# GRU gates of a fused graph network: h_n and i_n as four 64x64 corner matmuls

## The chip, the cores and the metric

The kernel runs on one core of a Trainium2 chip. The metric is the device time of one execution in microseconds: 815.14 us, the median of three runs (815.1 to 816.52). The profiled execution spans 813.9 us.

## The reference

A graph of 4096 nodes with 64 features each, and a 4096 x 4096 adjacency matrix of zeros and ones, passes through four layers. Each layer computes `x = x + layer(relu(layernorm(x)), adj)`. Layers 0, 1 and 3 are a decayed neighbour sum, a hyperbolic attention and a hyperbolic midpoint. The change lies in layer 2, which applies a gated graph convolution twice:

```
m = adj @ (x @ W)
gi = m @ wih.T + bih
gh = x @ whh.T + bhh
i_r, i_z, i_n = jnp.split(gi, 3, axis=-1)
h_r, h_z, h_n = jnp.split(gh, 3, axis=-1)
r = jax.nn.sigmoid(i_r + h_r)
z = jax.nn.sigmoid(i_z + h_z)
n = jnp.tanh(i_n + r * h_n)
return (1.0 - z) * n + z * x
```

The gates r and z need the sum of a product with x and a product with m. The candidate n needs the two products apart, because r multiplies only h_n.

## The kernel before, in words

The nodes are cut into four quarters of 1024. The adjacency matrix stays on the chip in fp8. It is converted while layer 0 runs; a check of the fp32 original (the tile `whole`, function `checks`) goes along on VectorE in the background through layers 0 to 2, because the fast path holds only for zeros and ones.

The program consists of the streams of the four layers and of chains of small operations between them. `stream0` ends at about 280 us and `stream1` at about 494. `layer2` runs twice: step 0 to about 602 us, step 1 to about 705. `layer3` ends on TensorE at about 793, and a tail on VectorE and ScalarE follows.

In `layer2` the sum adj @ x is made for each quarter, with x split into three bf16 parts (`hm` holds two of them side by side, `lo` the third). The multiplication with W is folded into the gate weights by `load_gates` once per step. `take2` then places the result m beside x: the tile `mx[0]` has x on partitions 0 to 63 and m on 64 to 127 for one chunk of 512 nodes, and `mx[1]` has them the other way round for the other chunk. `gates` (line 1509) makes the GRU of one quarter from these two tiles. So it is called eight times, four quarters by two steps.

The weight tile `gw` has for each chunk four blocks of 64 columns, for r, z, h_n and i_n. Its 128 rows meet the rows of `mx`, so that one matmul adds the product with x and that with m. For h_n the rows that meet m are zero, and for i_n those that meet x are zero (`pack_consts` leaves these blocks at zero). A gate is therefore two matmuls with 128 rows and 64 columns, one per chunk; the first writes partitions 0 to 63 of the result, the second 64 to 127. The tile `rz` holds r in its first bank and z in its second, the tile `ih` holds i_n in its first and h_n in its second.

The order of the work is made at build time by a planner, `Weave`. Each chain is a generator that yields operations; each operation is booked on a model of its engine with an estimated duration. While the sums of `layer2` are emitted, `draw` looks which yielded operations could begin by the model, and places them there. A chain goes on to its next operation only when the one before is placed. `book_pe` (line 964) holds the estimates for TensorE: a matmul that uses only half of the rows or columns is booked at half the time, and a switch between such matmuls and full ones gets a surcharge. The hardware queues then run in the emitted order and wait on semaphores.

In `gates` the order of the chain is: first gate r, then h_n (line 1526), then the sigmoid for r on ScalarE (1528), then gate i_n (1529) and gate z (1530), then on VectorE `(h_n + b) * r` and the addition of i_n (1531 and 1532), then the sigmoid for z, the tanh and the blend with x.

Of the kernel before, what the change touches and what calls it, by code (L numbers as in the profile page):

```python
# [18 lines left out]
P = 128  # L19
D = 64  # L20
NH = 2
CW = 512
# [578 lines left out]
def names(*aps):  # L601
    return [a.tensor.name for a in aps if isinstance(a, bass.AP)]


class Weave:
# [52 lines left out]
    def free(self, ps):  # L658
        k = ps.tensor.name
        self.banks[self.kind.pop(k)].append(self.used[k][0])  # L660
# [131 lines left out]
def fast_kernel(ctx: ExitStack, tc: tile.TileContext, t: dict, out: bass.AP, flag: bass.AP):  # L792
# [30 lines left out]
    def two(name):  # L823
        return weave.take(2, lambda: psp.tile([P, 2 * CW], F32, tag="two", name=name, bufs=2))
# [4 lines left out]
    def b2(name, shape=(P, QB, D), dtype=F32):  # L829
        return b2p.tile(list(shape), dtype, tag="b2", name=name)  # L830
# [57 lines left out]
    def w(name, a=0, b=None):  # L888
        s = L.at[name]
        return W[:, s.start + a:s.stop if b is None else s.start + b]  # L890
# [73 lines left out]
    def book_pe(o, lhsT, rhs, passes):  # L964
        k, m, n = lhsT.shape[0], math.prod(lhsT.shape[1:]), math.prod(rhs.shape[1:])
        tiled = k < P or m < P
        dur = max(0.42e-3 * n * passes * (0.5 if tiled else 1.0), 0.09)
        if passes > 1 and not tiled:
            dur += 0.05 if passes == 2 else 0.075
        weave.book("P", dur + ((0.18 if passes == 4 else 0.115) if tiled != weave.tiled else 0.0), names(lhsT, rhs), names(o))  # L970
        weave.tiled = tiled

    def mm(o, lhsT, rhs, start=True, stop=True):
        weave.wait(names(lhsT, rhs), names(o))
        book_pe(o, lhsT, rhs, 4 if lhsT.dtype == F32 else 1)
        nc.tensor.matmul(o, lhsT, rhs, start=start, stop=stop, skip_group_check=True)  # L976

    def turn4(o, src):
        book_pe(o, src, ident, 2)
        nc.tensor.transpose(o, src, ident)  # L980

    def PE(ins, run, dur, kinds=()):
        return Op("P", dur, names(*ins), (), run, kinds)
# [525 lines left out]
    def gates(q, step):  # L1509

        lo, hi = slice(0, D), slice(D, P)
        mx, xT = state.pop((step, q))
        gw, gb = gate_w[step], w(f"gb{step + 1}")
        rz, ih = [None], [None]
        assert ("gates", step) in DONE

        def gate(ps, half, i):
            if ps[0] is None:
                ps[0] = two("rz" if ps is rz else "ih")
            o = ps[0][:, half * CW:(half + 1) * CW]  # L1520
            for c in (0, 1):
                k = (4 * c + i) * D
                mm(o[lo if c == 0 else hi, :], gw[:, k:k + D], mx[c])

        yield PE(mx, lambda: gate(rz, 0, 0), 0.9, [2, 2])
        yield PE(mx, lambda: gate(ih, 1, 2), 0.9, [2])
        r = b2("r", (P, CW))
        yield AC.activation(r, rz[0][:, :CW], AF.Sigmoid, bias=gate_b[:, 2 * step:2 * step + 1])
        yield PE(mx, lambda: gate(ih, 0, 3), 0.9)
        yield PE(mx, lambda: gate(rz, 1, 1), 0.9)  # L1530
        yield DV.scalar_tensor_tensor(r, ih[0][:, CW:], gb[:, 5:6], r, op0=ALU.add, op1=ALU.mult)
        yield DV.tensor_tensor(r, r, ih[0][:, :CW], ALU.add)
        free(ih[0])
        z = b2("z", (P, CW))
        yield AC.activation(z, rz[0][:, CW:], AF.Sigmoid, bias=gate_b[:, 2 * step + 1:2 * step + 2])
        free(rz[0])
        yield AC.activation(r, r, AF.Tanh, bias=gb[:, 2:3])
        yield DV.tensor_tensor(xT, xT, r, ALU.subtract)
        yield DV.tensor_tensor(xT, xT, z, ALU.mult)
        yield DV.tensor_tensor(xT, xT, r, ALU.add)  # L1540
        return xT

    def post2a(q):
        x = yield from gates(q, 0)
        yield AC.activation(x, x, AF.Relu)
        ps = yield from to_nm(x, 1 if q < NQ - 1 else 2)
        yield from split3(ps, 1.0, *parts(3, q))
        DONE.add((3, q))
        yield from spill2(q, 1, x)

    def post2b(q):
        o = yield from gates(q, 1)
        DONE.add(("gates", q))
        kind = 1 if q < NQ - 1 else 2

        def run():
            ps = bank(kind, "ps_o")
            for j in range(4):
                turn4(ps[:, j * P:(j + 1) * P], o[:, j * P:(j + 1) * P])
            return ps  # L1560
        ps = yield PE([o], run, 0.6, [kind])
        yield DV.scalar_tensor_tensor(X[q], blocks(ps), 0.0, X[q], op0=ALU.max, op1=ALU.add)
        free(ps)
        yield from pre3(q, kind)
# [321 lines left out]
```

## Time and profile before

| | |
|---|---|
| time, median of three | 815.14 us |
| TensorE busy (matmul) | 776.2 us, 95% |
| VectorE busy | 638.4 us, 78% |
| ScalarE busy | 397.4 us, 49% |
| instructions of gate matmuls (rz and ih) | 64 and 64, 128*64, 128x512 f32 |
| busy time of rz and ih | 16.8 and 15.3 us |

A line of the profile names the engine (PE is TensorE's matmuls, PEld its weight loads, ACT ScalarE, DVE VectorE, SP the queue that issues transfers), the source line, the operation, and "out<-in" with the tiles' names. For a matmul "128*64" stands for the rows and columns of the weights in use. Line 976 is the helper that issues every matmul, and 781 the one for all VectorE and ScalarE operations, so the tile names tell them apart. In the view over time the first two numbers are the start and the length in microseconds; brackets hold the idle time before the operation and what ended it. An fp32 matmul appears as two instructions. Matmuls overlap in the pipeline, so the distance between starts says more than the lengths.

### The profile page before, as it was taken

How to read it: one execution, taken by the hardware profiler on the slowest of the kernel's cores; microseconds unless marked ns; L12 is line 12 of the kernel's file. 1: busy time of each engine (PE TensorE's matmuls, PEld its weight loads, DVE VectorE, ACT ScalarE, POOL GpSimd, SP SyncE). 2: the span in 40 equal slices, each digit the busy share in tenths (PEclk: the TensorE clock that was granted, in tenths of full speed). 3: DMA queues.
4: the chain of work that ended last, by engine and by line, in shares of the span. 5: the costliest groups of instructions: out<-in, count | busy, mean ns of one | idle time of the engine just before them, and what ended most of it. 6: DMA issues, size and time to landing. Idle time of an engine off the chain costs nothing.

```text
span 813.9 us, 12101 instructions
## 1 busy us (share of the span) xinstructions
PE 776.2 (95%) x4473; PEld 358.6 (44%) x4494; DVE 638.4 (78%) x1433; ACT 397.4 (49%) x613; POOL 61.1 (8%) x125
## 2 busy tenths in 40 slices
PE   5999999999999999999999999999999999999990
PEld 1334444444433333333333334444444444699990
DVE  6886777677678798888888888878779787774896
ACT  5655555565565657666666663022120254452333
POOL 3333232230000000000000000000000000000000
PEclk9999999999999999999999999999999999999995
DMA  9999999998301032022022016797879900000010
GB/s 220 151 176 168 201 160 192 196 161 186 104 14 39 0 118 65 0 91 65 0 66 91 0 33 239 287 319 229 283 263 356 273 23 4 2 2 1 2 41 17
DMA packets 43954, 98.39 MB, mean 121 GB/s; under 512 B 5104, under 2 KB 20464, under 8 KB 43888
## 3 DMA queue, kind: packets, MB, share of 16 engines
q1 hardware_dynamic: 25888, 78.98, 29.0%
q0 software_dynamic: 15840, 14.42, 18.9%
q10 hardware_dynamic: 2160, 4.14, 1.4%
q8 instruction: 37, 0.61, 0.3%
q14 instruction: 29, 0.24, 0.1%
HBM read 135.54 MB, written 5.24 MB: 173 GB/s over the span
## 4 chain that ended last, share of the span: by engine, by line
PE 90%; DVE 6%; ACT 1%; issue 1%; DMA 1%; SPq 0%; DVEq 0%; ACTq 0%
PE acc L976 54%; PE cnt L976 14%; PE score L976 14%; PE rz L976 2%; DVE sig L781 2%; PE ih L976 1%; PE ps_t L980 1%; PE ps_l L976 1%; DMA whole<-in_adjT 1%; PE ps_kq L976 1%; DVE ss L781 1%; DVE nt L781 1%; ACT sig L781 1%; PE ps_n L980 1%; DVE rc L781 0%
## 5 line engine op out<-in xcount | busy, mean ns | idle before, releaser
L781 ACT ACTIVATE sig<-score,fatt_add,fatt_mul 128x1024 f32<-128x1024 f32 x128 | 147.9, 1200 | 85.4 <-PE score L976 84.8
L781 DVE TENSOR_TENSOR sig<-sig,A 128x1024 f32<-128x1024 f32 x128 | 151.3, 1221 | 38.7 <-ACT sig L781 37.9
L781 DVE SCALAR_TENSOR_TENSOR whole<-whole 128x1024 f32<-128x1024 f32 x128 | 153.2, 1218 | 6.0 <-DMA whole<-in_adjT 5.6
L781 ACT ACTIVATE w<-cnt 128x512 int16<-128x512 f32 x198 | 111.2, 595 | 89.9 <-PE cnt L976 88.7
L976 PE MATMUL score<-qd,kT 64*128 64x512 f32 x512 | 128.2, 617 | 0.0
L976 PE MATMUL acc<-sig,S 128*64 128x512 f32 x512 | 125.4, 606 | 1.5 <-DVE sig L781 1.4
L976 PE MATMUL acc<-A,hm 128*128 128x512 fp8e4 x512 | 115.6, 379 | 0.8 <-DVE X L781 0.8
L976 PEld LDWEIGHTS <-hm 128*128 128x128 bf16 x768 | 73.5, 98 | 90.7 <-issue 10.5
L976 PE MATMUL cnt<-A,ftri 128*128 128x512 fp8e4 x256 | 97.9, 385 | 8.3 <-ACT A L781 8.3
L976 PE MATMUL cnt<-A,fupd 128*128 128x512 fp8e4 x248 | 95.6, 386 | 2.7 <-DVE w L781 1.6
L976 PE MATMUL acc<-S,A 128*128 128x196 bf16 x1024 | 88.2, 246 | 0.0
L976 PEld LDWEIGHTS <-A 128*128 128x128 fp8e4 x1024 | 87.1, 96 | 1.1 <-issue 0.8
L976 PEld LDWEIGHTS score<-qd,kT 64*128 64x128 f32 x512 | 43.7, 186 | 80.9 <-ACT sig L781 39.1
L781 DVE TENSOR_SCALAR w<-cnt 128x512 int16<-128x512 f32 x58 | 40.1, 691 | 45.5 <-PE cnt L976 41.1
L976 PE MATMUL acc<-w,hm 128*128 128x512 bf16 x235 | 71.0, 379 | 0.9 <-issue 0.2
L860 POOL DMA_DIRECT2D A<-in_adjT x110 | 59.3, 541 | 119.7 <-DMA A<-in_adjT 118.8
L976 PEld LDWEIGHTS acc<-sig,S 128*64 128x64 f32 x512 | 30.4, 136 | 82.7 <-issue 39.5
L976 PEld LDWEIGHTS <-lo 128*64 128x64 bf16 x768 | 36.9, 109 | 58.4 <-issue 36.4
L976 PE MATMUL acc<-A,lo 128*64 128x512 fp8e4 x512 | 59.3, 380 | 0.0
L781 ACT ACTIVATE mt<-acc 64x512 f32<-64x512 f32 x32 | 18.9, 591 | 66.2 <-PE acc L976 39.6
L976 PEld LDWEIGHTS <-fupd 128*128 128x128 bf16 x248 | 24.4, 98 | 46.0 <-issue 24.3
L1647 POOL MEMSET S<- 128x4 bf16 x8 | 0.9, 116 | 550.6 <-PE ps_l L976 505.4
(185 smaller groups left out, 649.5 us busy)
## 6 DMA issues: line engine op xcount, KB each, us to landing
whole<-in_adjT SPq DMA_DIRECT2D x128, 512.0 KB, 7.0
A<-in_adjT POOLq DMA_DIRECT2D x110, 128.0 KB, 13.2
qd<-qs SPq DMA_DIRECT2D x16, 128.0 KB, 3.0
mx<-gs SPq DMA_DIRECT2D x16, 128.0 KB, 8.1
xT<-gs SPq DMA_DIRECT2D x8, 256.0 KB, 7.6
x<-in_x SPq DMA_DIRECT2D x6, 256.0 KB, 6.1
xs<-x SPq DMA_DIRECT2D x4, 256.0 KB, 4.8
qs<-qT ACTq DMA_DIRECT2D x4, 256.0 KB, 6.3
```

Source lines behind the costliest of these rows:

```text
L781: return fn(*args, **kw)
L860: nc.gpsimd.dma_start(A8[q][b // 2][:, b % 2, :], a)
L976: nc.tensor.matmul(o, lhsT, rhs, start=start, stop=stop, skip_group_check=True)
L980: nc.tensor.transpose(o, src, ident)
L1647: nc.gpsimd.memset(S3[q, c][:, :, 3 * e:], 1.0)
```

## The change

h_n and i_n are no longer made with the zero rows. Each is now a product of 64 rows (those of x alone, or those of m alone) with 64 columns. Two gates by two chunks give four such matmuls: their inputs lie on the lower or the upper 64 partitions, and so do their outputs, and the four take all four combinations. The function `news` issues them one after the other in one step of the chain, ahead of the sigmoid for r, and the separate step for i_n disappears. The intention is that the four corners of the array work at the same time. `book_pe` now books a matmul with few rows and few columns at a quarter instead of half.

```
-        dur = max(0.42e-3 * n * passes * (0.5 if tiled else 1.0), 0.09)
+        dur = max(0.42e-3 * n * passes * (0.5 if tiled else 1.0) * (0.5 if k < P and m < P else 1.0), 0.09)
...
+        def news():
+
+            ih[0] = two("ih")
+            for c, (x, m) in enumerate(((lo, hi), (hi, lo))):
+                o = lo if c == 0 else hi
+                for own, half, i in ((x, 1, 2), (m, 0, 3)):
+                    k = (4 * c + i) * D
+                    mm(ih[0][o, half * CW:(half + 1) * CW], gw[own, k:k + D], mx[c][own, :])
+
         def gate(ps, half, i):
             if ps[0] is None:
-                ps[0] = two("rz" if ps is rz else "ih")
+                ps[0] = two("rz")
...
         yield PE(mx, lambda: gate(rz, 0, 0), 0.9, [2, 2])
-        yield PE(mx, lambda: gate(ih, 1, 2), 0.9, [2])
+        yield PE(mx, news, 0.9, [2])
         r = b2("r", (P, CW))
         yield AC.activation(r, rz[0][:, :CW], AF.Sigmoid, bias=gate_b[:, 2 * step:2 * step + 1])
-        yield PE(mx, lambda: gate(ih, 0, 3), 0.9)
         yield PE(mx, lambda: gate(rz, 1, 1), 0.9)
```

## The prediction, made before the result was known

> **What bounds the kernel now.** I read the busy shares first, then the chain that ended last, and then one gate call instruction by instruction.
>
> ```profile
> PE 776.2 (95%) x4473; PEld 358.6 (44%) x4494; DVE 638.4 (78%) x1433; ACT 397.4 (49%) x613; POOL 61.1 (8%) x125
> ...
> PE 90%; DVE 6%; ACT 1%; issue 1%; DMA 1%; SPq 0%; DVEq 0%; ACTq 0%
> PE acc L976 54%; PE cnt L976 14%; PE score L976 14%; PE rz L976 2%; DVE sig L781 2%; PE ih L976 1%; PE ps_t L980 1%; PE ps_l L976 1%; DMA whole<-in_adjT 1%; PE ps_kq L976 1%; DVE ss L781 1%; DVE nt L781 1%; ACT sig L781 1%; PE ps_n L980 1%; DVE rc L781 0%
> ```
>
> An average over stages settles nothing, so the next view cuts the span at layer 2 (494 to 602 and 602 to 705), layer 3 (to 793.2) and the tail. The first numbers are the length of the stretch and TensorE's busy time.
>
> ```profile
> 494.00:602.00 108.00, 108.00 (x635) 47.50 (x631) 87.41 (x161) 23.76 (x41) 0.00 (x0) 1.00 0.84 281
> 602.00:705.00 103.00, 101.73 (x626) 48.18 (x626) 84.30 (x212) 32.98 (x58) 0.46 (x4) 1.00 0.44 146
> 705.00:793.20 88.20, 88.18 (x1020) 86.85 (x1016) 66.17 (x266) 31.41 (x86) 0.47 (x4) 1.00 0.03 11
> ```
>
> TensorE is idle 1.3 us in the 211 us of layer 2 and not at all in layer 3, and the chain runs through the gate matmuls (rz, ih) themselves. So a microsecond taken from TensorE in layer 2 should come off the end, if it is not lost again in a wait. The eight gate calls start at 537, 548, 573, 597, 638, 649, 677 and 702 us. This is the first:
>
> ```profile
> 536.82 1.08 PE L976 MATMUL rz<-mx,g 128*64 128x512 f32 x4
> 537.72 1.89 PE L976 MATMUL ih<-mx,g 128*64 128x512 f32 x8
> 537.97 0.69 ACT L781 ACTIVATE r<-rz,gate_b 128x512 f32<-128x512 f32 x1 [3.51 <-PE rz L976]
> 539.44 1.03 PE L976 MATMUL rz<-mx,g 128*64 128x512 f32 x4
> 539.74 0.75 DVE L781 SCALAR_TENSOR_TENSOR r<-ih,W,r 128x512 f32<-128x512 f32 x1 [2.60 <-PE ih L976]
> 540.30 1.03 PE L976 MATMUL acc<-A,lo 128*64 128x512 fp8e4 x8
> ```
>
> An fp32 matmul shows as two instructions, so "ih x8" is four matmuls. Starts, not durations, tell the price, since the matmuls are pipelined: ih begins at 537.72 and the next group at 539.44, so two gates of two matmuls cost 1.72 us, 0.86 a gate. In that time two matmuls run side by side, one in each half of the columns.
>
> **What the Trainium skill says.** TensorEngine Tiling, "Tiling Modes": with 64 rows and 64 columns there are four tiles which work independently, twice as many as with 128 rows and 64 columns. The trace shows the pair form on the rows (score) and on the columns (rz, ih, lo), but no 64x64 matmul. The same section ("Key Properties") says that a change of tiling mode drains TensorE. The trace agrees and prices it, below. The same page, "Gotcha 1: PSUM Pressure", says that different row tiles cannot use the same PSUM bank at one time. Here each bank gets the top rows' result on one half of its partitions and the bottom rows' on the other; no run so far shows whether that counts as the same bank. TensorE: Matmul & The Clock Gate, "Measured speedup vs the span model", gives 10.6 times for sixteen 32x32 tiles at once, so packing in rows and columns together is not excluded.
>
> **The change, part by part.** *Removed:* in each call, h_n and i_n as four 128x64 matmuls, 1.72 us. Half of their weights are zeros, since h_n needs only the rows of x and i_n only those of m. *Added:* four 64x64 matmuls in the four corners, again 8 instructions of 512 columns. If all four run together this is one pair time, 0.86 us; if only two do, 1.72 us. I take 0.86: pairs in rows and pairs in columns each overlap fully in this trace, and each half of the partitions receives its two results in two different banks, as score's pair does.
>
> *Mode switches.* rz before and after stay 128x64, so the corners add a switch in and one out. Layer 1 shows what one costs, since it alternates two modes:
>
> ```profile
> 292.40 1.99 PE L976 MATMUL score<-qd,kT 64*128 64x512 f32 x8
> 294.32 1.94 PE L976 MATMUL acc<-sig,S 128*64 128x512 f32 x8
> 296.18 1.99 PE L976 MATMUL score<-qd,kT 64*128 64x512 f32 x8
> ```
>
> Eight instructions should take 4 x 0.43 = 1.72 us at 0.43 a pair. Score to acc takes 1.92 and acc to score 1.86, so a switch costs 0.20 into 128-column weights and 0.14 into 64-column ones, part drain and part a first weight load that nothing hides (in the first call rz, just switched in, lasts 0.90 instead of 0.86: some 0.05 of load, so 0.10 of drain). Both new switches go to 64-column weights: 2 x 0.145 = 0.29. The bounds are 0, if this pair of modes doesn't drain, and 0.40. A clean call thus gains 0.86 - 0.29 = 0.57 us.
>
> *The wait that was hidden.* The second rz gate writes the other half of the tile that the sigmoid for r reads, and waits for that sigmoid. Two calls show it:
>
> ```profile
> 550.12 0.67 ACT L781 ACTIVATE r<-rz,gate_b 128x512 f32<-128x512 f32 x1
> 550.84 0.20 PEld L976 LDWEIGHTS rz<-mx,g 128*64 128x64 f32 x4 [0.80 <-ACT r L781]
> ...
> 678.26 1.28 ACT L781 ACT_TABLE_LOAD   x1 [2.79 <-PE rz L976]
> 679.56 0.69 ACT L781 ACTIVATE r<-rz,gate_b 128x512 f32<-128x512 f32 x1
> 680.30 1.08 PE L976 MATMUL rz<-mx,g 128*64 128x512 f32 x4 [0.44 <-ACT r L781]
> ```
>
> In the first call r runs from 537.97 to 538.66, and TensorE leaves rz at 537.72: 0.94 us, which must be covered by what stands between. Before, that was 1.72; after, it is the corners with their first switch, 0.145 + 0.86 = 1.00. It just suffices, by 0.06 and the second drain. Where ScalarE is late it doesn't: in the second call (ScalarE busy with split3 of the quarter before) r ends at 550.79, and in the seventh (a table load of 1.28 us) at 680.25. There the second rz starts where it starts now, so these two calls gain nothing. Everything behind it on TensorE, the lo matmuls of the next sum, waits along. The sixth call has i_n separate (r is late at 652.43 and the planner put other sums between); there the corners go with h_n and the gain stays.
>
> *Sum:* 6 calls x 0.57 = 3.4 us. Layer 2 has nothing else to hide it, layer 3 is TensorE from end to end, and the 20 us tail only moves. The update of r on VectorE starts about 0.7 us sooner (it waits for the last ih), and z 0.57 sooner; both hang from the gates, so the chain to the next layer shortens too. I count nothing for it, because TensorE has other sums meanwhile.
>
> *The planner's price* (book_pe): corners are booked at a quarter, 0.86 for four, without a switch. It costs nothing by itself, but the order of all later work is made from these bookings. In both steps the order of fills may shift by an operation, up to a microsecond either way by the trace (idle stretches of 1.0 at 672 and 0.6 at 680). The 128 input checks go along at their DMA's pace (7.0 us to land); five or so may slip behind, into layer 3, where VectorE is busy 66 of 88 us.
>
> **The rivals.** (a) *No switch price, or no late sigmoid:* 8 x 0.86 = 6.9 us, 808.3. For it: both modes have 64 columns. Against: every change of shape in the trace pays. Chance 0.12. (b) *The gain is swallowed:* the corners overlap, but the hidden wait appears in all calls or a shifted order opens idle stretches of about 3 us: 815. For it: the margin of 0.06 us, and ScalarE late in three of eight calls. Against: layer 2 has sums to fill with. Chance 0.15. (c) *Only two corners at a time*, because of the shared banks: 1.72 + 0.29 instead of 1.72, 8 x 0.29 = 2.3 us more, 817.4, slower than before. For it: the skill's sentence on banks, and no 64x64 matmul seen. Against: halves of partitions are as separate as in the column pairs, whose two results do share a bank. Chance 0.16.
>
> **How the numbers follow.** Forecast: 815.1 - 3.4 = 811.7, chance 0.57. Faster by over 0.2% (under 813.5) holds most of the forecast and all of (a): 0.54 + 0.12 and 0.02 of (b), 0.68. Within 0.2%: most of (b) and an edge of the forecast, 0.15. Slower: (c) and 0.01 of (b), 0.17. The range leaves out (c) and takes in (a) and (b): 808.2 to 816.2.
>
> **What would show it.** In the changed profile: an ih group of 64*64, four starts within some 20 ns and the group over after 0.86 (right) or in two rounds (c); 0.10 before and 0.05 inside at each switch; the second rz 1.0 us after the corners begin, and waits for r of up to 0.9 us in one to three calls; layer 2's TensorE time down by some 4.5 us, with a little more idle. A table load or split3 landing on more of the sigmoids would make me wrong towards (b).

## The result, and the profile after

The changed kernel takes 811.46 us (median of four runs, 811.07 to 812.75) against 815.26 us before: a ratio of 0.9953, interval 0.9936 to 0.997. A second comparison gave 811.49 against 816.47, ratio 0.9944 (0.9932 to 0.9957). Forecast were 811.7 us and a range of 808.2 to 816.2.

In some executions of one and the same kernel the clock granted to TensorE falls to half for 3.41 us in layer 1, which then takes 262.3 us instead of 260.6, so the medians of two groups of runs can differ by up to 1.7 us more or less than the kernels do. The profile before has no such stretch, the profile after has one from 292.4 to 295.8 us. In the same four microseconds, before and then after, the first bracket counts TensorE's matmuls, and the third number from the end is the granted clock as a share of full speed:

```profile
293.00:297.00 4.00, 4.00 (x20) 1.30 (x18) 3.14 (x4) 2.31 (x3) 0.00 (x0) 1.00 0.63 190
293.00:297.00 4.00, 4.00 (x14) 0.91 (x10) 2.17 (x4) 2.41 (x2) 0.00 (x0) 0.65 0.63 193
```

So I also count from the last matmul of layer 1 (494.3 us before, 495.4 after, by its start), which leaves this stretch out.

The page after, busy time and the chain that ended last:

```profile
PE 772.4 (95%) x4473; PEld 355.6 (44%) x4494; DVE 638.3 (79%) x1433; ACT 396.9 (49%) x613; POOL 60.9 (8%) x125
...
PE 85%; DVE 10%; issue 1%; ACT 1%; DMA 1%; SPq 0%; ACTq 0%; DVEq 0%
```

TensorE is busy 3.8 us less, although its layer 1 is 1.65 us longer; VectorE and ScalarE are busy as long as before. But the chain runs 10% through VectorE instead of 6%; the chain in order of time, before and then after, shows where it changes over:

```profile
734.99 23.63 PE acc L976 x278
758.74 34.46 PE acc L976 x404
793.22 0.28 ACT n L781
```

```profile
734.98 16.33 PE acc L976 x192
751.34 0.39 ACT n L781
...
752.71 2.30 DVE whole L781 x4
```

From 751 us on the changed kernel's end hangs on VectorE's queue, in which two input checks (`whole`) stand. Before, the chain stays on TensorE up to 793. The first gate call after, over time:

```profile
537.99 1.08 PE L976 MATMUL rz<-mx,g 128*64 128x512 f32 x4
538.99 1.09 PE L976 MATMUL ih<-mx,g 64*64 64x512 f32 x8
539.14 0.69 ACT L781 ACTIVATE r<-rz,gate_b 128x512 f32<-128x512 f32 x1 [3.51 <-PE rz L976]
540.01 1.08 PE L976 MATMUL rz<-mx,g 128*64 128x512 f32 x4
540.92 1.25 PE L976 MATMUL acc<-A,lo 128*64 128x512 fp8e4 x10
```

From the start of rz to that of lo it is 2.93 us, against 3.48 before: 0.55 less. The eight instructions of the corners start in two rounds of four, each round within 21 ns (538.994 to 539.014 and 539.474 to 539.495), so all four run at once. The second and the seventh call, corners and second rz:

```profile
547.75 1.09 PE L976 MATMUL ih<-mx,g 64*64 64x512 f32 x8
549.46 1.08 PE L976 MATMUL rz<-mx,g 128*64 128x512 f32 x4 [0.62 <-ACT r L781]
...
675.05 1.09 PE L976 MATMUL ih<-mx,g 64*64 64x512 f32 x8
677.28 1.08 PE L976 MATMUL rz<-mx,g 128*64 128x512 f32 x4 [1.14 <-ACT r L781]
```

Here rz follows the start of the corners after 1.71 and 2.23 us instead of 1.02, because it waits for the sigmoid. These two calls take 3.62 and 4.09 us from the first rz to its successor, and took 3.63 and 4.09 before: nothing is gained. From the starts, the eight calls sum to 25.5 us instead of 28.8, 3.3 us less.

That is not all. Between the last matmul of layer 1 and the last of layer 3 the change takes off 4.8 us (298.7 to 293.9), and the tail behind it grows from 20.9 to 21.4. So 1.4 us on TensorE need another explanation, and the tail does not only move, it also grows.

### The profile page after: what moved, and what is told of

It reads as the page before. It is cut to its first block, busy times and chain, and to the rows that moved or that the text cites. A ratio compares the mean times of both kernels' runs of the same rounds, so it can differ in the third digit from the quotient of the medians.

```text
span 810.7 us, 12099 instructions
## 1 busy us (share of the span) xinstructions
PE 772.4 (95%) x4473; PEld 355.6 (44%) x4494; DVE 638.3 (79%) x1433; ACT 396.9 (49%) x613; POOL 60.9 (8%) x125
## 4 chain that ended last, share of the span: by engine, by line
PE 85%; DVE 10%; issue 1%; ACT 1%; DMA 1%; SPq 0%; ACTq 0%; DVEq 0%
PE acc L976 51%; PE score L976 14%; PE cnt L976 13%; DVE n L781 2%; PE rz L976 2%; DVE sig L781 2%; PE ps_t L980 1%; PE ps_l L976 1%; DVE ss L781 1%; DMA whole<-in_adjT 1%; DVE nt L781 1%; PE ps_kq L976 1%; PE ih L976 1%; ACT sig L781 1%; PE ps_n L980 1%
```

## The experiments

The theory: the corners save 0.55 us in six calls, the wait for the sigmoid takes back what they save in the other two, and the planner's new order brings the 1.4 us that are left. The rival: the order makes the gain. The columns are TensorE's part from the last matmul of layer 1 to the last of layer 3, the tail behind it (both in the profiled run), input checks that VectorE runs behind the sigmoid for z of the eighth call ("late checks"), the median, and its ratio to the kernel before with the interval. The kernel before had medians of 816.71, 816.47 and 816.42 us in the three groups of runs.

| kernel | TensorE | tail | late checks | median | ratio |
|---|---|---|---|---|---|
| before | 298.7 | 20.9 | 1 | 815.26 | |
| changed | 293.9 | 21.4 | 2 | 811.46 | 0.9953 (0.9936 to 0.997) |
| wide_same_order | 297.2 | 21.6 | 2 | 815.44 | 0.9989 (0.9983 to 0.9996) |
| corners_twice | 299.2 | 21.7 | 2 | 818.15 | 1.0018 (1.0012 to 1.0025) |
| corners_old_price | 301.9 | 19.3 | 0 | 818.8 | 1.0035 (1.0025 to 1.0046) |
| z_gate_early | 292.3 | 27.0 | 7 | 816.53 | 0.9993 (0.9985 to 1.0001) |
| changed_again | 293.9 | 21.4 | 2 | 811.49 | 0.9944 (0.9932 to 0.9957) |
| z_early_same_order | 294.6 | 21.6 | 2 | 813.68 | 0.9964 (0.9951 to 0.9977) |
| corners_first_same_order | 299.7 | 21.4 | 2 | 817.14 | 1.0016 (1.0008 to 1.0024) |
| z_gate_early_7_fewer | 292.3 | 27.0 | 0 | 816.23 | 0.9997 (0.9989 to 1.0005) |
| z_gate_early_7_unbooked | 292.4 | 19.6 | 0 | 809.25 | 0.9906 (0.9891 to 0.9922) |
| corners_first_planned | 292.5 | 19.3 | 0 | 808.0 | 0.9903 (0.9887 to 0.9918) |
| old_price_z_early | 301.1 | 19.6 | 0 | 816.47 | 1.0002 (0.9992 to 1.0011) |
| i_n_after_sigmoid | 295.1 | 21.7 | 2 | 812.79 | 0.9963 (0.9949 to 0.9977) |

In two of these profiles a stretch at half clock lies behind layer 1 and so within TensorE's part: in corners_old_price from 706.4 us on, where it costs about 1.7 us by the starts, and in old_price_z_early from 684.9 us on, about 1.4 us.

**wide_same_order** takes the corners away and keeps the order:

```diff
-                    mm(ih[0][o, half * CW:(half + 1) * CW], gw[own, k:k + D], mx[c][own, :])
+                    book_pe(ih[0][o, half * CW:(half + 1) * CW], gw[own, k:k + D], mx[c][own, :], 4)
+            for half, i in ((1, 2), (0, 3)):
+                for c, o in enumerate((lo, hi)):
+                    k = (4 * c + i) * D
+                    nc.tensor.matmul(ih[0][o, half * CW:(half + 1) * CW], gw[:, k:k + D], mx[c],
...
```

> Order and planner bookings are those of the changed kernel; only the four corners are again four 128-row matmuls (1.72 us, no mode switch). Theory (the corners themselves save 0.55 us in the six clean calls and nothing in the two calls where the second rz waits for the late sigmoid): 6 x 0.55 = 3.3 us more than changed, 814.8, and the other 0.5 us of the whole gain is the planner's order. Rival (the gain came mostly from the new order, fewer mode switches and a vanished idle stretch of 1 us): about 812.

```profile
538.12 1.08 PE L976 MATMUL rz<-mx,g 128*64 128x512 f32 x4
539.02 1.89 PE L1528 MATMUL ih<-mx,g 128*64 128x512 f32 x8
540.74 1.03 PE L976 MATMUL rz<-mx,g 128*64 128x512 f32 x4
541.60 0.60 PE L976 MATMUL acc<-A,lo 128*64 128x512 fp8e4 x4
```

The call takes its 3.48 us again. TensorE's part is 3.3 us longer than in the changed kernel, as the theory had it: that is the corners' share, measured in one and the same order. The other 1.4 us between this kernel and the kernel before are the order's. Most of it is an idle stretch in the kernel before that is gone, 1.0 us by the starts:

```profile
667.36 3.84 PE L976 MATMUL acc<-A,hm 128*128 128x512 fp8e4 x17
672.04 3.40 PE L976 MATMUL acc<-A,hm 128*128 128x512 fp8e4 x15 [0.83 <-DVE X L781]
```

Layers 2 and 3 also have 42 mode switches instead of 46.

**corners_twice** issues the four corners again behind the first set, unbooked:

```diff
+            for c, (x, m) in enumerate(((lo, hi), (hi, lo))):
...
+                    nc.tensor.matmul(ih[0][o, half * CW:(half + 1) * CW], gw[own, k:k + D], mx[c][own, :],
```

> The four corners are issued a second time behind the first, with no booking, so the order stays. Theory (four at once, 0.86 us a set; the wait for the late sigmoid of 0.78 and 1.30 us in calls two and seven absorbs the second set): 6 x 0.86 + 0.08 + 0 = 5.2 us more, 816.7. Rival without absorption: 8 x 0.86 = 6.9 us, 818.4. Rival of two at a time: 8 x 1.72 = 13.8 us, 825.

```profile
537.69 1.09 PE L976 MATMUL ih<-mx,g 64*64 64x512 f32 x8
538.60 1.04 PE L1529 MATMUL ih<-mx,g 64*64 64x512 f32 x8
539.57 1.08 PE L976 MATMUL rz<-mx,g 128*64 128x512 f32 x4
```

In this call a second set costs 0.86 us, without a switch. TensorE's part is 5.3 us longer for 5.2 expected, and the rivals' 6.9 and 13.8 are far off. The median, 818.15, lies near the first rival's 818.4, but the profiled run, whose layer 1 has no stretch at half clock, took 817.06. Both ends of the theory hold: four at once, and two calls in which the second set lies in the sigmoid's wait.

**i_n_after_sigmoid** leaves order and bookings, but issues the i_n pair with z:

```diff
-                    mm(ih[0][o, half * CW:(half + 1) * CW], gw[own, k:k + D], mx[c][own, :])
+                    book_pe(ih[0][o, half * CW:(half + 1) * CW], gw[own, k:k + D], mx[c][own, :], 4)
+            pair(1, 2, (lo, hi))
...
+        def last():
+            pair(0, 3, (hi, lo))
+            gate(rz, 1, 1)
...
-        yield PE(mx, lambda: gate(rz, 1, 1), 0.9)
+        yield PE(mx, last, 0.9)
```

> Order and bookings of the changed kernel, but the two corners of i_n are issued with z, behind the place of the sigmoid, as i_n was before the change. Theory (what matters is that the four stand next to each other in TensorE's queue, which they do in seven calls; in the sixth the i_n pair runs alone and pays 0.5 to 0.9 us): changed plus 0.5 to 0.9. Rival (two pairs issued apart run one after the other): changed plus 0.86 in each of six to seven calls, 5 us or more.

```profile
537.66 1.09 PE L1530 MATMUL ih<-mx,g 64*64 64x512 f32 x8
...
646.06 1.08 PE L1530 MATMUL ih<-mx,g 64*64 64x512 f32 x4
648.92 1.08 PE L1530 MATMUL ih<-mx,g 64*64 64x512 f32 x4
```

In the first call the four still run together, although h_n and i_n are separate steps; in the sixth, where other sums stand between, each pair costs a full round. TensorE's part is 1.2 us longer, somewhat over the 0.5 to 0.9 expected, since the second pair brings its own round and switch. So "issued together" matters only as neighbourhood in TensorE's queue, and is worth 1.2 us.

**corners_old_price** books the corners at half, as the rule before did:

```diff
-        dur = max(0.42e-3 * n * passes * (0.5 if tiled else 1.0) * (0.5 if k < P and m < P else 1.0), 0.09)
+        dur = max(0.42e-3 * n * passes * (0.5 if tiled else 1.0), 0.09)
```

> Corners as changed, but booked at half instead of a quarter, so that only the planner's order differs. Theory (the matmuls make the gain, the order about 1 us either way): 811 to 812.5. Rival (the order makes it): 814 or more. To be seen as well: whether the idle stretch of 1.0 us ahead of the seventh call is back.

The theory fell: with the very same matmuls the kernel is slower than the kernel before. The idle stretch ahead of the seventh call is not back, but there are new ones. The second rz gates in calls six, seven and eight (the last lasts 1.65 us because the clock falls to half in it):

```profile
650.78 1.08 PE L976 MATMUL rz<-mx,g 128*64 128x512 f32 x4 [1.64 <-ACT r L781]
...
679.93 1.08 PE L976 MATMUL rz<-mx,g 128*64 128x512 f32 x4 [2.24 <-ACT r L781]
...
706.00 1.65 PE L976 MATMUL rz<-mx,g 128*64 128x512 f32 x4 [2.92 <-ACT r L781]
```

Believing in 0.86 us more of TensorE time, the planner put more of ScalarE's other work ahead of the sigmoid (a square in calls six and eight, a table load of 1.28 us in seven and eight). TensorE is idle 7.4 us behind layer 1, against 1.8 in the changed kernel. Whether these waits alone make it slow was tried in **old_price_z_early**, with z ahead of the corners in the same order; beside the price, its edit is that of z_early_same_order below:

> Order and bookings of corners_old_price, but the z matmuls stand ahead of the corners, so that nothing waits for the sigmoid. Theory (corners_old_price loses 0.78 + 1.80 + 2.41 + 3.09 us in such waits, against 2.1 in changed): most of that comes back, 4 to 6 us under corners_old_price, 813 to 815. Rival (the planner's other placements make it slow): 817 or more.

TensorE's part fell by 0.8 us only, the ratio from 1.0035 to 1.0002. The waits for the sigmoid went, and others of 1.8, 2.9 and 2.0 us came, at transposes and at the flag matmul (which sums up the input checks). So the rival is nearer: these waits are not the cause by themselves, since without them TensorE waits elsewhere in that plan. That the plan is bad because its price is wrong is not shown. wide_same_order speaks against it as a rule: it runs 1.72 us of work in places booked at 0.86, and is 1.4 us shorter on TensorE than the kernel before, which books these matmuls at what they take.

**z_early_same_order** and **corners_first_same_order** take the wait out of the changed kernel, its order held: z's matmuls move ahead of the corners, or the corners ahead of r and z.

```diff
+            for c in (0, 1):
+                nc.tensor.matmul(rz[0][lo if c == 0 else hi, CW:], gw[:, (4 * c + 1) * D:(4 * c + 2) * D], mx[c],
...
-        yield PE(mx, lambda: gate(rz, 1, 1), 0.9)
+        yield PE(mx, book_z, 0.9)
```

> Emitted order and bookings are those of the changed kernel, except that the two z matmuls stand ahead of the corners and so ahead of the sigmoid for r, which no matmul waits for any longer. Theory (the waits of 0.78 and 1.30 us in calls two and seven are pure loss, and the chain is not longer, since it waits for the corners in any case): 2.1 us less than changed, tail as in changed. Rival (the sigmoid, 0.86 us later, delays the chain, and TensorE waits elsewhere): no less than changed.

```diff
+            corners(raw)
+            gate(raw, 0, 0)
+            gate(raw, 1, 1)
+            gate(book, 0, 0)
...
-        yield PE(mx, lambda: gate(rz, 0, 0), 0.9, [2, 2])
-        yield PE(mx, news, 0.9, [2])
+        yield PE(mx, first, 0.9, [2, 2])
+        yield PE(mx, lambda: corners(book), 0.9)
...
-        yield PE(mx, lambda: gate(rz, 1, 1), 0.9)
+        yield PE(mx, lambda: gate(book, 1, 1), 0.9)
```

> As z_early_same_order, but the corners stand ahead of r and z. In the four calls that follow full 128x128 matmuls and are followed by 128x64 ones (one, two, five, six) this makes two mode switches out of three. Theory: 4 x 0.145 = 0.6 us less than z_early_same_order, 2.6 us less than changed. Rival (r and z come 1.0 us later, the chain is longer and the sums beside it don't cover that): 0 to 1 us more than z_early_same_order.

**changed_again** is the changed kernel itself, run beside these two:

> The changed kernel once more, so that the three beside it have the same base: 0.9953 of the kernel before, about 3.8 us less.

It took 811.49 us, 0.9944 of the kernel before. Against it the two reorderings lose 2.2 and 5.7 us by their medians; TensorE's part and tail together, which leave the stretch in layer 1 out, are 0.9 and 5.8 us longer.

Both expectations failed. The rivals hold in direction, but corners_first_same_order is 5.1 us longer on TensorE than z_early_same_order, where its rival had 0 to 1. In the first call of z_early_same_order the update of r waits for the last ih, which now ends 0.93 us later, and so does all that hangs from it, up to the transposes:

```profile
539.57 0.75 DVE L781 SCALAR_TENSOR_TENSOR r<-ih,W,r 128x512 f32<-128x512 f32 x1 [2.72 <-PE ih L976]
...
544.28 0.63 ACT L781 ACTIVATE xT<-xT 128x512 f32<-128x512 f32 x1 [1.25 <-DVE xT L781]
...
545.12 0.63 PE L980 MATMUL ps_n<-fident,xT 128*128 128x128 f32 x4 [0.32 <-DVE mx L781]
```

In changed_again the same lines stand at 538.64, 543.34 and 544.62 us, and the transposes wait for nothing. The line names mx, but xT ends at 544.91, so it is xT that ended last. The chain has about 0.45 us of slack there. A delay of 0.93 uses it up and leaves TensorE idle: six such stretches of 0.3 to 0.7 us, 0.7 us more in sum than the sigmoid's waits were. With the corners first, everything in the chain comes later by another round: eight stretches of 0.6 to 1.2 us.

**z_gate_early** lets the planner place the order r, z, corners, sigmoid:

```diff
         yield PE(mx, lambda: gate(rz, 0, 0), 0.9, [2, 2])
+        yield PE(mx, lambda: gate(rz, 1, 1), 0.9)
         yield PE(mx, news, 0.9, [2])
...
-        yield PE(mx, lambda: gate(rz, 1, 1), 0.9)
```

> Order r, z, corners, then the sigmoid for r: no matmul any longer stands behind the sigmoid. Theory (waits of 0.78 and 1.30 us are all that is lost to it, and the sums beside the chain hide its later start): 2.1 us less than changed, 809.4. Rival (the sigmoid starts 0.86 us later, so the chain to the next layer is longer and the idle time appears elsewhere): 811 to 812.

TensorE's part falls by 1.6 us: both waits for the sigmoid are gone, and one stretch of 0.7 us at 667 us is left. But the tail grows by 5.7, and the median, 816.53, is above what theory and rival said. Seven checks stand at 749 to 758 us on VectorE instead of two. **z_gate_early_7_fewer** leaves these seven instructions out and keeps their bookings; **z_gate_early_7_unbooked** drops the bookings too.

```diff
+            if n > 121:
+                op.run = lambda op=op: weave.book("D", op.dur, op.ins, op.outs)
+            yield op
```

> z_gate_early with the last seven of the 128 checks left out of the VectorE queue (their loads and bookings stay, so all else is in the same order): the check covers less of the input. Theory (its 27.0 us tail, 5.7 over the changed kernel's, comes from seven checks of 1.22 us that the planner let slip to 749 us, in front of layer 3's last chains on VectorE): the tail falls to about 20 to 21, the time to 1.5 to 2.5 us under changed. Rival (the tail comes from the order of the chains themselves): 26 us or more stay.

```diff
+            if n > 121:
+                op.dur, op.run = 0.0, lambda: None
+            yield op
```

> z_gate_early with the last seven checks neither issued on VectorE nor booked by the planner (the check covers less of the input). Leaving out the instructions alone left the tail at 27.0 us, so the seven as such are not what makes it long. Theory (their bookings made the planner put the takes of the next sums ahead of the first chain of layer 3's end, and the in-order queues then wait there for TensorE): without the bookings the tail is 21 to 22 us and the time 1.5 to 2 us under changed, about 809.7. Rival (the order of the gates puts the tail off by another way): 26 us or more stay.

The first expectation failed: without 8.5 us of work in front, the tail is the same. ScalarE's queue in z_gate_early and then in z_gate_early_7_unbooked shows why:

```profile
750.80 0.28 ACT L781 ACTIVATE n<-acc 128x130 f32<-128x130 f32 x1 [2.27 <-PE acc L976]
753.52 0.28 ACT L781 ACTIVATE n<-acc 128x130 f32<-128x130 f32 x1 [2.38 <-PE acc L976]
756.24 0.28 ACT L781 ACTIVATE n<-acc 128x130 f32<-128x130 f32 x1 [2.38 <-PE acc L976]
...
767.39 1.28 ACT L781 ACT_TABLE_LOAD   x1
```

```profile
750.51 0.39 ACT L781 ACTIVATE n<-acc 128x260 f32<-128x260 f32 x1 [2.38 <-PE acc L976]
752.51 0.42 ACT L781 ACTIVATE sq<-n 128x256 f32<-128x256 f32 x1 [1.55 <-DVE n L781]
754.38 0.42 ACT L781 ACTIVATE sq<-n 128x256 f32<-128x256 f32 x1 [1.45 <-DVE n L781]
756.25 0.42 ACT L781 ACTIVATE sq<-n 128x256 f32<-128x256 f32 x1 [1.45 <-DVE n L781]
...
756.91 1.28 ACT L781 ACT_TABLE_LOAD   x1
```

With the seven booked, the planner takes VectorE for occupied and puts the copies of the next sums out of PSUM (n<-acc) ahead of the first closing chain (sq<-n, table load). In the real queues these copies wait for TensorE, up to 2.4 us each, and the chain behind them reaches its table load at 767.4 us instead of 756.9; in z_gate_early_7_fewer it is 767.3. Unbooked, the tail is 19.6 us and the time 809.25.

**corners_first_planned** has the corners, r, z, and then the sigmoid, placed by the planner:

```diff
-        yield PE(mx, lambda: gate(rz, 0, 0), 0.9, [2, 2])
-        yield PE(mx, news, 0.9, [2])
+        yield PE(mx, news, 0.9, [2, 2])
+        yield PE(mx, lambda: gate(rz, 0, 0), 0.9, [2])
+        yield PE(mx, lambda: gate(rz, 1, 1), 0.9)
...
-        yield PE(mx, lambda: gate(rz, 1, 1), 0.9)
```

> Corners, r, z, then the sigmoid, placed and booked by the planner in this order (corners_first_same_order kept the places of another order). Theory (no wait for the sigmoid, fewer mode switches, and the planner, which knows of the later chain, puts the next transposes where they are ready; no check slips into layer 3): TensorE's part 2 us under changed with the tail of changed, about 809.5. Rival (the chain is 1.0 us longer whatever the planner does): 812 or more.

It takes 808.0 us, ratio 0.9903, and leaves nothing out: faster than both kernels. TensorE's part is 1.4 us shorter than in the changed kernel, where I expected 2 (the mode switches are as many, 58, and one idle stretch of 0.8 is left), and the tail is 2.1 shorter, which I did not expect. The same order of matmuls in a plan made for another one, corners_first_same_order, is among the three slowest.

## Why the prediction was right, point by point

*Four corners in one round, 0.86 us:* right. Each round of four starts within 21 ns, and a second set costs 0.86. The sentence of the Trainium skill on row tiles and one bank (TensorEngine Tiling, "Gotcha 1: PSUM Pressure") does not bind in this case, where the two row tiles write different halves of the partitions: rival (c) had 2.3 us more, and the changed kernel takes 3.8 less.

*Switches, 0.29 us a call:* right. The first call went from 3.48 to 2.93, 0.86 less 0.31. That a drain is paid between 128x64 and 64x64 too agrees with the same page's "Key Properties": the starts lie 0.10 us further apart going into the corners and 0.11 going out of them.

*The hidden wait:* right, in the two calls named and in no other. The seventh call's wait, 1.14 us, is longer than the 0.9 that was allowed for; since its second rz starts when the sigmoid ends, the sum does not change by that.

*Sum of 3.4 us:* right, 3.3 by the starts of the eight calls and 3.3 by wide_same_order.

*The planner's order, up to a microsecond either way:* mis-sized. It brought 1.4 us here. With the old price the same matmuls take 8.0 us more on TensorE: 5.7 in idle stretches, 1.7 in the stretch at half clock, the rest about what five more mode switches cost. The new booking is thus a part of the change that I priced at almost nothing. How much of such a difference lies in the right price and how much in the chance of one plan or another stays open, since only two prices were tried.

*The chain counts for nothing, TensorE has other sums:* wrong as a general step. The sums are placed at build time, and what follows waits in the queue. The gates' chain has some 0.45 us to spare in its first call of the changed kernel, and the 0.93 us that z_early_same_order adds leave TensorE idle. What the earlier start was worth within the change itself no run separates.

*The tail only moves, and late checks find room on VectorE:* wrong, with a small effect here: two late checks instead of one, 0.4 us more tail. Over the kernels with all their checks, the tail is 19.3 to 19.6 us with no late check, 20.9 with one, 21.4 to 21.7 with two, 27.0 with seven. For seven the cause is shown: the bookings, and not the instructions. For one and two it is read from the pattern and the chain, not tried.

The forecast of 811.7 thus came from the right term. Two that it lacked, 1.4 us less and 0.4 us more, make it 4.3 us from layer 1 on by the profiled runs, and the medians differ by 3.8 and 5.0 in the two comparisons. That the forecast lies within 0.3 us of the median is in part luck: nothing in it stood for the order's 1.4 us, which lies beyond the microsecond that it allowed for.

## What to carry to other kernels

Pack small matmuls by rows and columns where the zeros of a block matrix allow it, and price it from starts: one round for four, less two mode switches, and nothing in those places where the next matmul waits for another engine anyway. Where an order is fixed at build time by estimated durations, every change of an estimate or of a chain draws a new order: with the same corner matmuls, no check left out and none doubled, the medians here lie between 808.0 and 818.8 us. So measure a change with the order held, as wide_same_order does, or the order's effect passes for the change's. No run here has the corners in the order of the kernel before. Removing a wait in a fixed order can cost more than it saves if the chain behind it has less slack than the operations moved.

## What was new about the hardware

In this kernel four 64x64 fp32 matmuls run at once even though each PSUM bank is written by the top rows on one half of the partitions and by the bottom rows on the other. They may stand in the queue as two separate pairs: the first starts of all four still lie within 20 ns (537.659 to 537.679 us in i_n_after_sigmoid). A mode switch adds 0.09 to 0.11 us between starts in the pairs of shapes timed here. From one round of fp32 matmuls to the next it is 0.43 us without a switch, 0.53 between score and acc and from rz into the corners, and 0.54 out of the corners; from one fp8 matmul of 128*128 to the next it is 0.22 us, and to the first of 128*64 0.31.

A stretch at half clock lasts 3.41 us and costs 1.4 to 1.7 us of TensorE time where matmuls fill it. The two that lie behind layer 1 begin within 0.4 us of the end of the two longest idle stretches of TensorE there in any run, 2.92 us in corners_old_price and 2.69 in old_price_z_early. That suggests that a long wait can cost more than its own length; no run was made to show it.
